# Group-norm statistics at the head of a fused attention and depthwise-convolution kernel: statistics split in two parts, more load buffers, small sums moved

## The chip, the cores and the metric

The kernel runs on one core of a Trainium2 chip. The metric is the device time in microseconds (us) of one execution, and lower is better. A profile describes one execution on the chip. Its engines are PE (TensorE, matrix products; PEld is its weight load), DVE (VectorE), ACT (ScalarE), POOL (GpSimd) and SP (SyncE, which here only starts transfers).

## What is computed

An image x of 384 channels and 192 x 192 pixels, float32, goes through two residual layers. The change lies in the first one, in the group norm and the first products behind it.

```python
# layer 0
n = groupnorm(x)                       # 32 groups of 12 channels, eps 1e-5
qkv = einsum('bchw,oc->bohw', n, w_qkv) + b_qkv      # 384 -> 1152 channels
qkv = maxpool 2x2 of qkv               # 96 x 96
qkv = depthwise 3x3 conv(qkv, w_dw) + b_dw
q, k, v = split(qkv)                   # 8 heads of 48 channels
attn = normalize(q) @ normalize(k).T * temperature   # 48 x 48 for each head
out = sum over 4 of topk_softmax(attn, kk) @ v * a
x = x + (w_proj @ upsample 2x(gelu(out)) + b_proj)
# layer 1
w_sym = mean of the four rotations of weight (7 x 7)
x = x + depthwise 7x7 conv(groupnorm(x), w_sym)
```

## The kernel before

The 384 channels are three tiles of 128 partitions (`KT`, index `kt` or `ct`). The image is cut into `NB` = 24 blocks of 8 rows (`BLK` = 1536 pixels). A group of 12 channels lies across the border between the second and the third tile, so the second tile's norm needs 8 channels of the third (`OVER`); these are loaded apart, spread over all partitions, as `xe`.

The norm is never applied to x. Its scale `rstd0` is multiplied into the rows of the weights `wq` (each row belongs to an input channel), and its mean becomes a bias: `biases` multiplies the scaled weights by `mean0` with TensorE and makes `negb` and `bdb`, which pooling borders and the depthwise taps need.

**Stage 1, statistics.** x is streamed once. For each block, `summed` (L310) runs six `bn_stats` instructions on VectorE for the first two tiles together. Blocks go from 23 down to 0. The last three (`NX`) land in `held` buffers, which are kept for stage 2; all others go through the pool `xsp` with three buffers. Then `bn_aggr` (L359) makes channel means and variances of all 24 blocks, and small matmuls against 0/1 matrices (`total`, L316) sum them over groups: first the group means (`gs_mid`, results `mids`), then moments about them (`gs`, from `ds`), from which `normed` makes `rstd0`; POOL takes the power -1/2 (L335). ScalarE scales the first two tiles of `wq` (L382). Only then the third tile's blocks are streamed in the same way, in pairs; its last block, 0, is kept apart from the aggregate of the 23 others.

**Begun products.** While the third tile's statistics run, TensorE multiplies the first two tiles of the kept blocks by the scaled weights: 24 sums of 512 pixels (`begun_qk`, L389), each two matmuls, each matmul two instructions in the trace[...]. Twenty are parked in SBUF by ScalarE (L395), the last four stay in their PSUM buffers. When the third tile's `rstd0` is there, VectorE scales the first third of its weights (L433) and ScalarE the rest (L434).

**Stage 2, q and k.** For each block, `pooled` (L553) makes the products, VectorE takes the 2 x 2 maximum into a ring of rows (L561) and runs nine taps for each tile (L601, L603), and `products` transposes and sums q by k (L621, L630). For block 0 and a part of block 1 only the third tile's product is added to the begun sums. `biases` is called after the first two tiles of block 0. POOL writes expanded 7 x 7 weights to memory meanwhile (`weights`), behind the third `rstd0`. Stage 3 makes v, the attention and the projection (L816, L903, L927), stage 4 the 7 x 7 convolution with matmuls (L1332 to L1343).

Order. A tile framework places every instruction on its engine's queue; each engine works through its queue in order. `tc.keep_in_program_order` pins matmuls to the order of the program, otherwise the planner chooses, by when it thinks that operands are there; `tc.issue_after(i)` holds an instruction behind another. The small sums over weights (`sumd` L442, `w7h` L171, `w7s` L174 and L177, `sumw` L1230) have nothing in their code that holds them back, and the planner put them among the first statistics on VectorE. SP starts the x loads, ScalarE the weight loads. A load also waits until the earlier load that used the same of eight completion semaphores has landed.

Of the kernel before, what the change touches and what calls it, by code (L numbers as in the profile page):

```python
# [13 lines left out]
P = 128  # L14
C = 384
# [63 lines left out]
def conv_preact_d2(  # L79
# [91 lines left out]
    nc.vector.tensor_tensor(w7h, w7f, w7f[:, :, ::-1], ALU.add)  # L171
    w7hv = w7h.rearrange("p t (a b) -> p t a b", b=KS)
    for i in range(KS):
        nc.vector.tensor_tensor(  # L174
            w7s[:, :, i, :], w7hv[:, :, i, :], w7hv[:, :, :, KS - 1 - i], ALU.add
        )
    nc.vector.tensor_scalar_mul(w7s, w7s, 0.25)  # L177
# [76 lines left out]

    psx = ExitStack()
# [29 lines left out]
    with tc.tile_pool(name="stp", bufs=1) as stp, tc.tile_pool(name="xsp", bufs=3) as xsp:  # L285
# [4 lines left out]
        xe = stp.tile([P, EN], F32, name="xe")  # L290
# [15 lines left out]
        nc.gpsimd.memset(whole[:, 0:OVER], 0.0)  # L306

# [4 lines left out]
        def total(name, n, terms):  # L312

            ps = ptr.tile([P, C], F32, name=name, tag="tr")
            for i, (lhs, rhs) in enumerate(terms):
                nc.tensor.matmul(ps[:, 0:n], lhs, rhs, start=(i == 0), stop=(i == len(terms) - 1))  # L316
            return ps[:, 0:n]
# [4 lines left out]
        def moments(dst, mv, mid):  # L322

            nc.vector.tensor_tensor(dst[:, 0:1], mv[:, 0:1], mid, ALU.subtract)
            nc.vector.tensor_tensor(dst[:, 1:2], dst[:, 0:1], dst[:, 0:1], ALU.mult)
            nc.vector.tensor_tensor(dst[:, 1:2], dst[:, 1:2], mv[:, 1:2], ALU.add)

        def normed(kt, ps, mid):
# [5 lines left out]
            nc.vector.scalar_tensor_tensor(rstd, g[:, 1:2], GN_EPS, rstd, ALU.add, ALU.subtract)  # L334
            last = nc.gpsimd.tensor_tensor(rstd, rstd, halfneg[:, 0:1], ALU.pow).ins  # L335
            nc.vector.tensor_tensor(mean0[:, kt : kt + 1], mid, g[:, 0:1], ALU.add)
            return last

        for b in reversed(range(NB)):
            if b < NX:  # L340
                xb = held[b][:, 0:TWO]
            else:
                xb = xsp.tile([P, TWO, BLK], F32, name=f"xs{b}", tag="xs")
# [6 lines left out]
        mv = stp.tile([P, KT, 2], F32, name="mv0")  # L350
        mve = stp.tile([P, 2], F32, name="mve")
        mids = stp.tile([P, KT + 1], F32, name="mids0")
        ds = stp.tile([P, KT, 2], F32, name="ds0")
        de = stp.tile([P, 2], F32, name="de")
        me = stp.tile([P, 1], F32, name="me")
        nc.vector.bn_aggr(mve, ste.rearrange("p n s -> p (n s)"))
        nc.vector.tensor_scalar_mul(me, mve[:, 0:1], 1.0 / EP)
        for kt in range(TWO):
            nc.vector.bn_aggr(mv[:, kt, :], st[:, kt].rearrange("p n s -> p (n s)"))  # L359
        means = [mv[:, kt, 0:1] for kt in range(TWO)]  # L360
        terms = [
            [(sel(0, 0), means[0]), (sel(1, 0), means[1])],
            [(sel(0, 1), means[0]), (sel(1, 1), means[1]), (shared[:, 0:P], me)],
            [(of, means[1]), (ones, me)],
        ]
        for k, i in ((0, 0), (1, 1), (KT, 2)):
            ps = total(f"gs_mid0_{k}", 1, terms[i])
            nc.vector.tensor_scalar_mul(mids[:, k : k + 1], ps, 1.0 / GC)
        for kt in range(TWO):
            moments(ds[:, kt], mv[:, kt], mids[:, kt : kt + 1])  # L370
        moments(de, mve, mids[:, KT : KT + 1])
        nc.vector.tensor_scalar_mul(de, de, 1.0 / EP)
        terms = [
            [(sel(0, 0), ds[:, 0]), (sel(1, 0), ds[:, 1])],
            [(sel(0, 1), ds[:, 0]), (sel(1, 1), ds[:, 1]), (shared[:, 0:P], de)],
# [3 lines left out]
        nc.vector.tensor_copy(chmean[:, 0:TWO], mv[:, 0:TWO, 0])  # L379
# [3 lines left out]
        keep = tc.keep_in_program_order  # L383
        for i, (b, ct, g) in enumerate(begun_qk):
# [14 lines left out]

        kt = TWO
        for b in [*range(NB - 2, NX, -2), NX, *reversed(range(1, NX))]:
            n = 2 if b > NX else 1
            if b < NX:
# [4 lines left out]
            nc.sync.dma_start(xb, xv[:, kt, b * BLK : (b + n) * BLK])  # L410
            summed(kt, b, n, xb)
        loaded = nc.sync.dma_start(held[0][:, kt], xv[:, kt, 0:BLK]).ins
        mvm, mvl = [stp.tile([P, 2], F32, name=f"mv0_{i}") for i in range(2)]
        dm, dl = [stp.tile([P, 2], F32, name=f"ds0_{i}") for i in range(2)]
        mid = mids[:, kt : kt + 1]
        nc.vector.bn_aggr(mvm, st[:, kt, SUB:, :].rearrange("p n s -> p (n s)"))
        ps = total(
            "gs_mid0_2", 1,
            [(sel(1, 2), means[1]), (shared[:, P:], me), (whole, mvm[:, 0:1])],
        )  # L420
        nc.vector.tensor_scalar_mul(mid, ps, 1.0 / GC)
        moments(dm, mvm, mid)
        nc.vector.tensor_scalar_mul(dm, dm, (NB - 1) / NB)
        summed(kt, 0, 1, held[0][:, kt])
        nc.vector.bn_aggr(mvl, st[:, kt, 0:SUB, :].rearrange("p n s -> p (n s)"))
        moments(dl, mvl, mid)
        nc.vector.scalar_tensor_tensor(ds[:, kt], dl, 1.0 / NB, dm, ALU.mult, ALU.add)
        ps = total(
# [995 lines left out]
```

## Time and profile before

| | us |
|---|---|
| median of 3 runs | 2841.81 |
| lowest and highest run | 2838.41, 2848.71 |
| the profiled execution | 2858.62 |
| its span, first to last instruction | 2856.9 |
| VectorE waits for wd, for w7t | 8.29, 4.48 |
| aggregates of all 24 blocks begin | 119.86 |
| first begun product on TensorE | 132.14 |
| last begun product ends | 175.34 |
| TensorE continues with the third tile | 182.45 |
| biases reach VectorE | 197.10 |
| mean granted TensorE clock | 0.983 |

Times below the span's row are counted from the start of the span, in the profiled execution. In the page, "busy" is the time in which an engine had an instruction under way; a line such as `L310 DVE` names line 310 of the kernel before and the engine. A bracket behind an instruction is the idle time before it and what ended it. In tables by stretches, each engine has its busy time and, in brackets, its instructions; the last three columns are the granted TensorE clock as a share of full speed, the busy share of the 16 DMA engines, and GB/s.

### The profile page before, as it was taken

To read this page: it belongs to the slowest core of one execution; us is meant where nothing else is said; L and a number is where in the kernel's file an instruction comes from. 1 tells how busy PE (TensorE), PEld (TensorE's weight loads), DVE (VectorE), ACT (ScalarE), POOL (GpSimd) and SP (SyncE) were. 2 spreads that over 40 slices of the span, in tenths; PEclk is the share of its full clock that TensorE was granted. 3 is DMA by queue.
4 is the path that set the end of the run, shared out by engine and by line. 5 is a ranking of instruction groups with operands and counts; after the bars stand their busy time and mean duration, and the time that the engine had idled before them with its cause. 6 is when DMAs were issued, how large, how long until landed. Compare 5 with 4: busy or idle time off the path is not lost.

```text
span 2856.9 us, 25452 instructions
## 1 busy us (share of the span) xinstructions
PE 2651.4 (93%) x8669; PEld 1585.7 (56%) x8669; DVE 2359.4 (83%) x3380; ACT 870.5 (30%) x1635; POOL 750.3 (26%) x874
## 2 busy tenths in 40 slices
PE   0299999999999999999899999999999699999997
PEld 0144444444445444444556656666666477777776
DVE  6979887887878878778688887888889679888886
ACT  0031111111111111111202232232323467777775
POOL 1024443100000000000102230010101467878785
PEclk9999999999999999999999999999999799999999
DMA  8886666301101011000335998576675899999997
GB/s 331 357 293 240 223 225 217 134 33 57 43 34 66 34 52 48 34 33 1 134 101 184 332 366 283 178 240 197 210 243 193 299 321 357 371 370 367 372 367 244
DMA packets 236401, 584.52 MB, mean 205 GB/s; under 512 B 16704, under 2 KB 168112, under 8 KB 219504
## 3 DMA queue, kind: packets, MB, share of 16 engines
q1 hardware_dynamic: 175344, 286.77, 29.2%
q0 software_dynamic: 37376, 148.85, 15.1%
q10 hardware_dynamic: 23552, 147.27, 13.7%
q8 instruction: 69, 1.13, 0.2%
q14 instruction: 60, 0.49, 0.0%
HBM read 374.47 MB, written 208.21 MB: 204 GB/s over the span
## 4 chain that ended last, share of the span: by engine, by line
PE 87%; DVE 6%; DMA 5%; POOL 1%; issue 1%; ACT 0%; SPq 0%; ACTq 0%; POOLq 0%; DVEq 0%
PE pq L553 36%; PE pv L816 19%; PE pc L1332 6%; PE pc L1343 6%; PE pc L1337 6%; PE pr L927 4%; PE po L903 3%; DMA xs<-in_x_dram 2%; PE grams L630 2%; PE tr L621 2%; DVE qk L603 2%; PE pq_begun L389 2%; DVE st L310 1%; DMA xv<-in_x_dram 1%; DVE vb L850 1%; DMA sd<-sx 1%
## 5 line engine op out<-in xcount | busy, mean ns | idle before, releaser
L553 PE MATMUL pq<-xq,wq 128*128 128x512 f32 x2268 | 990.7, 592 | 0.0
L553 PEld LDWEIGHTS pq<-xq,wq 128*128 128x128 f32 x2268 | 422.9, 190 | 492.2 <-issue 446.1
L603 DVE SCALAR_TENSOR_TENSOR qk<-ring,wd,qk 128x384 f32<-128x384 f32 x1152 | 674.0, 612 | 20.9 <-ACT ring L590 7.1
L816 PE MATMUL pv<-xv,wq 128*128 128x384 f32 x1728 | 567.0, 488 | 10.6 <-DMA xv<-in_x_dram 9.3
L816 PEld LDWEIGHTS pv<-xv,wq 128*128 128x128 f32 x1728 | 328.5, 191 | 238.2 <-DVE rows L822 8.6
L561 DVE TENSOR_REDUCE ring<-pq 128x128 f32<-128x512 f32 x428 | 293.7, 687 | 192.3 <-PE pq L553 191.7
L1356 DVE TENSOR_SCALAR apart<-pc,rb 32x576 f32<-32x576 f32 x384 | 312.2, 813 | 87.1 <-PE pc L1343 65.5
L1354 ACT ACTIVATE apart<-pc,rb 32x576 f32<-32x576 f32 x384 | 281.4, 733 | 143.0 <-PE pc L1343 138.2
L850 DVE SCALAR_TENSOR_TENSOR vb<-rows,wd,vb 128x576 f32<-128x576 f32 x384 | 313.1, 817 | 11.2
L1343 PE MATMUL pc<-aux,h 128*128 128x288 f32 x768 | 250.7, 408 | 3.5 <-POOL aux L1265 2.7
L1332 PE MATMUL pc<-main,w 128*128 128x288 f32 x768 | 251.9, 409 | 0.9 <-issue 0.3
L961 DVE TENSOR_TENSOR sx<-xr,y 128x576 f32<-128x576 f32 x192 | 217.6, 1174 | 41.0 <-ACT y L935 23.9
L1337 PE MATMUL pc<-main,w 128*128 128x288 f32 x768 | 250.7, 408 | 0.0
L612 ACT ACTIVATE junk<-qk 128x384 f32<-128x384 f32 x144 | 75.3, 523 | 540.9 <-DVE qk L603 540.9
L1302 POOL COPY res<-apart 128x1152 f32<-128x1152 f32 x96 | 224.0, 2361 | 40.9 <-ACT apart L1354 27.8
L713 POOL MEMSET lower<- 128x2304 f32 x1 | 2.0, 2018 | 871.3 <-PE grams L630 871.3
L1002 POOL DMA_DIRECT2D sd<-sx x96 | 72.3, 756 | 512.5 <-DVE sx L961 491.1
L822 DVE TENSOR_REDUCE rows<-pv 128x192 f32<-128x768 f32 x144 | 137.5, 955 | 64.6 <-PE pv L816 64.6
L1343 PEld LDWEIGHTS pc<-aux,h 128*128 128x128 f32 x768 | 145.7, 190 | 47.0 <-POOL aux L1265 3.5
L1332 PEld LDWEIGHTS pc<-main,w 128*128 128x128 f32 x768 | 145.5, 191 | 44.9 <-PE pc L1343 2.7
L1197 DVE SCALAR_TENSOR_TENSOR w<-eye,sb,w 128x512 f32<-128x512 f32 x96 | 168.8, 1797 | 1.5
L1337 PEld LDWEIGHTS pc<-main,w 128*128 128x128 f32 x768 | 146.5, 191 | 41.9
(210 smaller groups left out, 2321.0 us busy)
## 6 DMA issues: line engine op xcount, KB each, us to landing
sd<-sx POOLq DMA_DIRECT2D x96, 600.0 KB, 10.0
xv<-in_x_dram SPq DMA_DIRECT2D x144, 384.0 KB, 4.9
xr<-in_x_dram SPq DMA_DIRECT2D x48, 1152.0 KB, 14.8
out_dram<-res SPq DMA_DIRECT2D x192, 288.0 KB, 11.4
main<-sd ACTq DMA_DIRECT2D x46, 1200.0 KB, 10.0
xq<-in_x_dram SPq DMA_DIRECT2D x21, 2304.0 KB, 8.5
w<-wt ACTq DMA_DIRECT2D x46, 1024.0 KB, 7.0
xs<-in_x_dram SPq DMA_DIRECT2D x24, 1536.0 KB, 8.5
```

The costliest lines, as they stand in the source:

```text
L553: nc.tensor.matmul(ps, wq[:, kt, ct * P : (ct + 1) * P], rows[:, kt, :, g * 64 : (g + 1) * 64], start=(kt == 0), stop=(kt == KT - 1), skip ...
L561: nc.vector.tensor_reduce(t[:, r0 : r0 + PR, 1 + g * 32 : 1 + (g + 1) * 32], ps.rearrange("p (h a w b) -> p h w a b", h=PR, a=2, b=2), AX. ...
L603: nc.vector.scalar_tensor_tensor(dst, src, w, dst, ALU.mult, ALU.add)
L816: nc.tensor.matmul(ps[:, u, 0 : RB * HW], wq[:, kt, o : o + P], xb[:, kt, u, :], start=(kt == 0), stop=(kt == KT - 1),)
L850: pin(nc.vector.scalar_tensor_tensor(dst, src, w, dst, ALU.mult, ALU.add))
L961: nc.vector.tensor_tensor(bass.AP(flat.tensor, flat.offset + at(e) + a * RUN, [flat.ap[0], [JP, NT], [1, NJ], [at(f) - at(e), 2]],), xq[:, ...
L1302: keep(nc.gpsimd.tensor_copy(res[:, k], apart[:, :, k].rearrange("p e n -> p n e")))
L1332: nc.tensor.matmul(acc, w[:, i, 0:P], main[:, i, :, 0:NJ], start=True, stop=False)
L1337: nc.tensor.matmul(acc, w[:, i, P : 2 * P], main[:, i, :, 1 : 1 + NJ], start=False, stop=False,)
L1343: nc.tensor.matmul(acc, h[:, i], aux[:, i, :, 0:NJ], start=False, stop=True,)
L1354: keep(nc.scalar.mul(dst, src, scale))
L1356: keep(nc.vector.tensor_scalar_mul(dst, src, scale))
```

## The change

- The statistics of the first two tiles are aggregated in two parts: the first 21 blocks before the last three are summed, then the last three alone. The group means that moments are taken about come from the first part; both parts' moments are weighted by their share of blocks and added. The third tile does the same (21 and 3 blocks instead of 23 and 1).
- `xsp` has five buffers instead of three, and `xe` uses one of them instead of its own.
- The sums of the 7 x 7 weights move from VectorE to POOL. `sumd`, `bpm` and `sumw` are held behind the third tile's last VectorE step of the norm (`settled`).
- All small matmuls of `total` are pinned, and the last 3 of the 24 begun sums come behind the third tile's group-mean matmuls.
- All three thirds of the third tile's weights are scaled by ScalarE, in three instructions.
- The bias products are split: after a zeroing matmul, those of q and k for the first two tiles (12 of 27) run before the third tile's scale is there; the rest stays in `biases`.
- The constants `z` and `zero` become one tile in another pool.

```diff
-    nc.vector.tensor_tensor(w7h, w7f, w7f[:, :, ::-1], ALU.add)
+    nc.gpsimd.tensor_tensor(w7h, w7f, w7f[:, :, ::-1], ALU.add)
...
-        nc.vector.tensor_tensor(
+        nc.gpsimd.tensor_tensor(
             w7s[:, :, i, :], w7hv[:, :, i, :], w7hv[:, :, :, KS - 1 - i], ALU.add
         )
-    nc.vector.tensor_scalar_mul(w7s, w7s, 0.25)
+    nc.gpsimd.tensor_scalar_mul(w7s, w7s, 0.25)
...
-    with tc.tile_pool(name="stp", bufs=1) as stp, tc.tile_pool(name="xsp", bufs=3) as xsp:
+    with tc.tile_pool(name="stp", bufs=1) as stp, tc.tile_pool(name="xsp", bufs=5) as xsp:
...
-        xe = stp.tile([P, EN], F32, name="xe")
+        xe = xsp.tile([P, TWO, BLK], F32, name="xe", tag="xs")
+        xe = xe.rearrange("p k n -> p (k n)")[:, 0:EN]
...
+        def aggregate(kt, lo, hi, name):
+
+            mv = stp.tile([P, 2], F32, name=f"mv0_{kt}_{name}")
+            nc.vector.bn_aggr(mv, st[:, kt, lo * SUB : hi * SUB, :].rearrange("p n s -> p (n s)"))
+            return mv
...
+        def both(kt, most, mid):
+
+            last = moments(aggregate(kt, 0, NX, "last"), mid, f"{kt}_last")
+            nc.vector.scalar_tensor_tensor(most, last, NX / NB, most, ALU.mult, ALU.add)
+            return most
...
         for b in reversed(range(NB)):
+            if b == NX - 1:
+                most[:TWO] = [aggregate(kt, NX, NB, "most") for kt in range(TWO)]
...
+                for k, i in ((0, 0), (1, 1), (KT, 2)):
+                    ps = total(f"gs_mid0_{k}", 1, terms[i])
+                    nc.vector.tensor_scalar_mul(mids[:, k : k + 1], ps, 1.0 / GC)
+                de = moments(mve, mids[:, KT : KT + 1], "e")
+                nc.vector.tensor_scalar_mul(de, de, 1.0 / EP)
+                dm = [moments(most[kt], mids[:, kt : kt + 1], f"{kt}_most") for kt in range(TWO)]
+                for d in dm:
+                    nc.vector.tensor_scalar_mul(d, d, rest0)
...
+        ds = [both(kt, dm[kt], mids[:, kt : kt + 1]) for kt in range(TWO)]
...
+        for i in range(len(spots) + 1):
+            begin(i)
...
-        for b in [*range(NB - 2, NX, -2), NX, *reversed(range(1, NX))]:
+        for b in [*range(NB - 2, NX, -2), NX, *reversed(range(NX))]:
             n = 2 if b > NX else 1
+            if b == NX - 1:
+                most = aggregate(kt, NX, NB, "most")
+                ps = total(
+                    "gs_mid0_2", 1,
+                    [(sel(1, 2), means[1]), (shared[:, P:], me), (whole, most[:, 0:1])],
+                )
+                nc.vector.tensor_scalar_mul(mid, ps, 1.0 / GC)
+                dm = moments(most, mid, "2_most")
+                nc.vector.tensor_scalar_mul(dm, dm, rest0)
+                for i in range(len(spots) + 1, len(begun_qk)):
+                    begin(i)
...
+        d = both(kt, dm, mid)
+        ps = total("gs0_2", 2, [(sel(1, 2), ds[1]), (shared[:, P:], de), (whole, d)])
+        stats0, settled = normed(kt, ps, mid)
...
+        bias_ps = ptr.tile([P, C], F32, name="bias_ps", tag="tr")
...
+        for ct in range(2 * KT):
+            for kt in range(TWO):
+                leave(ct, kt)
-    nc.vector.tensor_scalar_mul(wq[:, kt, 0:C], wq[:, kt, 0:C], rstd0[:, kt : kt + 1])
-    nc.scalar.mul(wq[:, kt, C:], wq[:, kt, C:], rstd0[:, kt : kt + 1])
+    for i in range(3):
+        w = wq[:, TWO, i * C : (i + 1) * C]
+        nc.scalar.mul(w, w, rstd0[:, TWO : TWO + 1])
...
-    nc.vector.tensor_reduce(sumd, wd, AX.X, ALU.add)
+    with tc.issue_after(settled):
+        nc.vector.tensor_reduce(sumd, wd, AX.X, ALU.add)
...
             for ct in range(CT):
-                for kt in range(KT):
...
+                for kt in range(TWO if ct < 2 * KT else 0, KT):
+                    leave(ct, kt)
```

`begin(i)` holds the body of the old loop over `begun_qk` (two matmuls, and the copy to SBUF for the first 20); `leave(ct, kt)` is one pinned bias matmul into `bias_ps`, accumulating. On VectorE the order after the change has no statistics between the first part's aggregates and its scaled moments, and the sums `sumd`, `bpm` and `sumw` stand just ahead of the first pooling; SP's order is the same.

## The prediction

> **What bounds the kernel now.** I read the page first, for the share of each engine and the 40 slices.
>
> ```profile
> span 2856.9 us, 25452 instructions
> ...
> PE 2651.4 (93%) x8669; PEld 1585.7 (56%) x8669; DVE 2359.4 (83%) x3380; ACT 870.5 (30%) x1635; POOL 750.3 (26%) x874
> ...
> PE   0299999999999999999899999999999699999997
> ```
>
> TensorE is busy in every slice but the first two and a few joints. A change that removes no matmul of weight can only move the moment from which TensorE runs without a pause. So the question is the first 200 us, and there the views by engine count. VectorE's timeline, which shows start, busy time, instruction and the idle time before it:
>
> ```profile
> 7.41 2.86 DVE L349 BATCH_NORM_STATS2 ste<-xe 128x6 f32<-128x384 f32 x6 [5.14 <-DMA xe<-in_x_dram]
> 18.57 0.24 DVE L442 TENSOR_REDUCE sumd<-wd 128x9 f32<-128x81 f32 x1 [8.29 <-DMA wd<-in_wdw_dram]
> ...
> 26.07 0.31 DVE L171 TENSOR_TENSOR w7h<-w7t 128x147 f32<-128x147 f32 x1 [4.48 <-DMA w7t<-in_w_dram]
> ...
> 104.99 14.95 DVE L310 BATCH_NORM_STATS2 st<-xs 128x6 f32<-128x512 f32 x24 [0.41 <-DMA xs<-in_x_dram]
> 119.86 4.05 DVE L359 BATCH_NORM_AGGREGATE mv<-st 128x2 f32<-128x432 f32 x2
> ```
>
> Two small sums over weights stand in VectorE's order ahead of the statistics of x, and it stood still 8.29 and 4.48 us for their transfers. No x buffer came free meanwhile. The table by stretches (the last two columns are the share of the 16 DMA engines and GB/s) shows what that cost:
>
> ```profile
> 18.50:28.70 10.20, 0.00 (x0) 0.00 (x0) 5.59 (x19) 1.28 (x1) 0.00 (x0) 1.00 0.49 162
> ...
> 40.00:50.00 10.00, 0.00 (x0) 0.00 (x0) 8.74 (x15) 0.00 (x0) 0.00 (x0) 1.00 1.00 393
> ...
> 100.00:110.00 10.00, 0.00 (x0) 0.00 (x0) 9.07 (x16) 0.00 (x0) 0.00 (x0) 1.00 1.01 420
> 110.00:120.00 10.00, 0.00 (x0) 0.00 (x0) 9.79 (x18) 0.00 (x0) 0.00 (x0) 1.00 1.02 425
> ```
>
> The loads stood half idle at 18.5 to 28.7; with three buffers they then ran at 378 to 405 GB/s, and at 420 to 425 only at the end, where three loads into the kept blocks need no buffer. The chain of waits (start, length) tells what follows:
>
> ```profile
> 98.17 18.09 DMA xs<-in_x_dram
> ...
> 119.94 3.98 DVE mv L359 x2
> ...
> 132.14 43.20 PE pq_begun L389 x96
> ...
> 182.45 5.88 PE pq_begun L553 x8
> ...
> 190.05 7.02 PE bias_ps L573 x50
> ```
>
> From the last load to the first product 15.9 us pass (116.26 to 132.14). The begun products end at 175.34, then TensorE waits for the third tile's statistics to 182.45, and the biases stand on it until 197.06. At 197.10 VectorE has the biases and starts its backlog of pooling and taps; TensorE has no gap beyond 0.94 us after that. So the mark that I compare is "biases on VectorE": 197.10 us. What it gains, the end gains.
>
> **The change part by part.**
>
> *Weight sums moved.* The sumd, w7h/w7s and sumw work leaves the head of VectorE's order. The w7 part goes to POOL, which is idle from 8.3 to 130.5 us and next does the power of the first rstd; nine small operations there after w7t lands (26 us) are 90 us early. sumd and sumw (0.24 and 0.30 us) come after the third rstd, where VectorE waits over 2 us for TensorE; at worst they reach 0.5 us into that wait. So VectorE stops only for x.
>
> *Five buffers.* They change nothing before 18.5 us: in both orders SP's second x load waits for xe to land and its third for a small bias load (11.1 us in the table of SP's waits), since both reuse a completion semaphore. xe now takes one of the five. Two x blocks have landed by 18.5 us (moved: 8 us at 284 and 10.5 us at 369 GB/s, 6.1 MB, the sum of xe, wq and two blocks). Block three, issued at 18.5, lands at about 24.5 (6 us for a single load, like xe's 6.6). From there I need the pace of an x block of 1.573 MB. Bounds: 4.02 us (the 20 blocks whose statistics end between 39.5 and 119.94 us) if buffers do not matter, 3.73 us (14.95/4, VectorE's own pace, met at 420 to 425 GB/s) if they do. I take 3.8, near the row with as many loads in flight.
>
> [...]
>
> *First statistics in two parts.* Of 24 blocks 21 are aggregated before the last three. Statistics of block 21 end at 24.5 + 3.7 + 18 x 3.8 = 96.6. Then VectorE works on the first part: two aggregates of 21/24 x 1.99 us (3.5), a wait for 12 TensorE instructions at 0.23 us (2.8; the 10 in this chain took 2.28), means, squares and scaling (1.3): 7.6 us with no statistics beside it. That is new on VectorE, and what queues behind it are the three last blocks; their loads go into kept buffers and are not delayed. 18 statistics of 0.61 us follow: 115.2. From there: two short aggregates (0.7; the 128x18 one took 0.23 and the 128x414 one 2.02), moments and weighting 0.75, 10 TensorE instructions 2.3, norm and rstd 0.6, POOL's power 0.6, ScalarE's scaling 0.95: begun products start at 121.2, against 132.14. That is 10.9 us, nearly all from the loads; the split itself cuts the tail from 12.2 to 6.0 us behind the last statistics and gives that back in the 7.6 us.
>
> *Third tile.* VectorE returns to statistics at 115.2 + 4.6 = 119.8; five blocks wait in the buffers by 123, so it is not held by loads. 63 + 1 statistics (39.0), an aggregate of 378 elements (1.85): its first part is ready at A = 160.7. TensorE has 21 of the 24 begun sums done at 121.2 + 38.0 = 159.2 and waits 1.5 us for A: a new stall, as the last three sums now stand behind this matmul. They take 5.2 us and end at A + 5.5; VectorE's remaining 8 statistics, aggregate and moments end at A + 6.4. Then gs (0.4), norm (0.55), power (0.6 with its wait), and ScalarE's first third (about 0.5; 0.93 for 768 columns): A + 8.6. The old step was VectorE's L433, 2.30 us, so moving it saves 1.8. In that gap TensorE now does 13 of the bias products, 26 instructions at 0.095 us (21 in 2 us at full clock, next fence): until A + 9.3. They fill the wait and overrun by 0.7.
>
> The clock, from the stretches again (column before DMA share):
>
> ```profile
> 180.00:182.00 2.00, 0.00 (x0) 0.00 (x0) 1.91 (x1) 0.93 (x1) 2.00 (x2) 0.51 0.00 0
> ...
> 190.00:192.00 2.00, 2.00 (x21) 2.00 (x19) 0.69 (x1) 1.13 (x2) 0.00 (x0) 1.00 0.98 293
> ...
> 194.00:196.00 2.00, 2.00 (x11) 2.00 (x10) 0.00 (x0) 0.00 (x0) 0.00 (x0) 0.50 1.00 285
> ```
>
> It fell 4.7 us after the last wide matmul (175.3) and again some 4 us into the bias products (189.9): small products do not hold it. My new gap without wide matmuls is 3.8 us (A + 5.5 to A + 9.3). [...] If it falls, 3.4 to 6.8 us at half speed cost 1.7 to 3.4 us. I charge nothing and keep 3.4 for the range.
>
> *Restart to biases.* Before 14.65 us (182.45 to 197.10): 12 matmuls, partly at half clock (5.88 + 1.72), and 50 bias instructions in 7.02. After: 12 x 0.43 = 5.2, then 30 instructions at 0.095 = 2.9: A + 17.4 = 178.1. TensorE's half clock until 200 us goes too, but VectorE bounds there: 0, at most 1.6.
>
> Costed at nothing: z and zero merged and moved (memsets before any data), the extra zeroing matmul (counted in the 26), chmean and bpm moved (VectorE waits there), SP's order (unchanged), POOL's first weight pieces (they start with the third rstd and shift along).
>
> **Sum.** First products 10.9 earlier; begun sums to restart 48.8 instead of 50.3 (1.5); restart to biases 8.1 instead of 14.65 (6.5): 19 us. The profiled execution took 2858.62 us (span 2856.9 and 1.7 around it), 16.8 over the median of 2841.81. The chain shows why: one x load of 26.69 us at 1692.89 made a round of the loop 63.9 us instead of 50.35. That is 13.5 us which the median need not hold; none of it is in the first 200 us. Rounding the gain to 18.5, the profiled one would give 2840 and the median 2823.
>
> **The rivals.**
> *Loads no faster (11%).* At 4.02 us a block, block 21 ends at 100.6: 4 us lost; with a clock drop at the restart, 3.4 more. Gain 11.6: 2830, within 0.5%. For it: the DMA share reads 1.00 already at 393 GB/s. Against: 425 with more in flight.
> *The head start is given back (4%).* TensorE reaches later blocks earlier, and if their xq loads or the backlog of VectorE held it, the gain would shrink to the bias part, 6.5 us: 2835. Against: the backlog's work is unchanged and starts when the biases do, and xq loads land in 8.5 us against a block of 51.
> *Slower (3%).* More loads in flight could disturb each other. All 34 blocks' worth after the second must land; with pace p the last does at 20.5 + 34p and the biases follow 13.9 us later, so the change loses from p = 4.8 us (328 GB/s), and loses 14 us at 5.2 (302 GB/s): 2856. No stretch between 40 and 120 us is under 378.
>
> **Numbers.** The likeliest case has 82%: 2823, own range 2817 to 2828 (pace 3.73 to 3.95, clock kept). About 0.5%, 14.2 us, is what a measurement of this kernel can tell from no change; the runs spread over 10 us. The border is 2827.6: of the likeliest case 4 of the 82 lie inside it, and so do the first two rivals: faster 0.78, same 0.19, slower 0.03. With the runs' spread, the range is 2813 to 2833.
>
> **What would show it.** Right: no VectorE wait on wd or w7t; DMA share at 1.0 from 20 us; first begun product near 121; a wait of 1 to 2 us before gs_mid's last product at 160; restart near 170 with the clock at 1.00; biases near 178; the same 51 us per block after. Wrong: block statistics still 4 us apart, begun products after 125, a clock of 0.5 at the restart, or a new TensorE gap between 180 and 260.

## The result and the profile after

The changed kernel takes 2823.41 us (median of 4 runs, 2822.68 to 2826.64) against 2842.36 us (median of 4, 2838.41 to 2848.71). The ratio is 0.9933, with a 95% interval of 0.9913 to 0.9953. The profiled execution has a span of 2822.3 us at a mean granted clock of 0.986.

First the page of the changed kernel: span, busy time of the engines, and TensorE's 40 slices.

```profile
span 2822.3 us, 25466 instructions
...
PE 2640.1 (94%) x8671; PEld 1581.2 (56%) x8671; DVE 2331.7 (83%) x3382; ACT 871.1 (31%) x1637; POOL 752.8 (27%) x884
...
PE   0399999999999999999899999999998699999997
```

TensorE is busy for nearly as long as before, 2640 us against 2651; what shrank is the time before it runs without a pause. VectorE's timeline of the changed kernel (start, busy time, instruction, idle time before it and what ended that):

```profile
26.08 3.66 DVE L318 BATCH_NORM_STATS2 st<-xs 128x6 f32<-128x512 f32 x6 [3.97 <-DMA xs<-in_x_dram]
30.00 14.95 DVE L318 BATCH_NORM_STATS2 st<-xs 128x6 f32<-128x512 f32 x24 [0.26 <-DMA xs<-in_x_dram]
46.02 52.58 DVE L318 BATCH_NORM_STATS2 st<-xs 128x6 f32<-128x512 f32 x84 [1.06 <-DMA xs<-in_x_dram]
98.51 3.56 DVE L337 BATCH_NORM_AGGREGATE mv_most<-st 128x2 f32<-128x378 f32 x2
...
105.85 10.77 DVE L318 BATCH_NORM_STATS2 st<-xs 128x6 f32<-128x512 f32 x18
116.54 0.64 DVE L337 BATCH_NORM_AGGREGATE mv_last<-st 128x2 f32<-128x54 f32 x2
...
120.71 37.47 DVE L318 BATCH_NORM_STATS2 st<-xt 128x6 f32<-128x512 f32 x63
...
158.69 1.84 DVE L337 BATCH_NORM_AGGREGATE mv_most<-st 128x2 f32<-128x378 f32 x1
...
180.45 0.17 DVE L624 TENSOR_TENSOR negb<-bias_ps,bq 128x9 f32<-128x9 f32 x1 [2.55 <-PE bias_ps L470]
```

No wait on wd or w7t is left. From 46.02 us on, 14 blocks pass in one piece at 3.76 us each, where before there was a wait of 0.3 to 1.1 us in every few blocks. The pause for the first part is 7.3 us (98.51 to 105.85). The third tile's 63 statistics run without a wait. The biases reach VectorE at 180.45 us instead of 197.10.

The loads behind it, in the table by stretches of the changed kernel:

```profile
18.50:28.70 10.20, 0.00 (x0) 0.00 (x0) 6.23 (x11) 1.28 (x1) 0.00 (x0) 1.00 0.84 304
...
40.00:50.00 10.00, 0.00 (x0) 0.00 (x0) 8.73 (x16) 0.00 (x0) 0.00 (x0) 1.00 1.02 416
100.00:110.00 10.00, 3.25 (x14) 3.13 (x14) 7.44 (x24) 0.00 (x0) 0.00 (x0) 1.00 1.02 426
```

304 GB/s stand where 162 were, and 416 where 393 were. TensorE's timeline of the changed kernel around the joint:

```profile
122.34 38.06 PE L423 MATMUL pq_begun<-xs,wq 128*128 128x512 f32 x84 [2.16 <-ACT wq L415]
...
160.90 5.40 PE L423 MATMUL pq_begun<-xs,wq 128*128 128x512 f32 x12
...
167.40 2.82 PE L470 MATMUL bias_ps<-mean,wq 128*128 128x1 f32 x24
170.08 5.38 PE L604 MATMUL pq_begun<-xs,wq 128*128 128x512 f32 x8
175.29 1.88 PE L604 MATMUL pq<-xs,wq 128*128 128x512 f32 x4
177.01 3.40 PE L470 MATMUL bias_ps<-mean,wq 128*128 128x1 f32 x30
180.28 8.81 PE L604 MATMUL pq<-xs,wq 128*128 128x512 f32 x16
```

Begun products start 9.8 us earlier and the third tile's product (the restart) 12.4 us earlier. But the eight instructions at 170.08 take 5.38 us, 0.67 each, where the 12 at the end of the begun sums took 0.45 each. The table by stretches of the changed kernel says why (third column from the right: granted clock):

```profile
168.00:170.00 2.00, 2.00 (x20) 2.00 (x20) 0.33 (x3) 1.44 (x3) 2.00 (x2) 1.00 0.00 0
170.00:172.00 2.00, 2.00 (x5) 0.96 (x6) 0.00 (x0) 0.19 (x1) 1.94 (x8) 0.57 0.00 0
172.00:174.00 2.00, 2.00 (x3) 0.72 (x3) 0.98 (x2) 0.59 (x1) 1.99 (x3) 0.58 0.32 94
...
180.00:182.00 2.00, 2.00 (x7) 0.97 (x7) 0.51 (x3) 1.35 (x6) 0.00 (x0) 0.63 0.99 299
182.00:184.00 2.00, 2.00 (x4) 0.91 (x3) 0.83 (x2) 2.00 (x8) 0.00 (x0) 0.52 1.00 285
```

The clock falls to half at the restart, for some 3.4 us, and again at 180.5. The prediction had charged nothing for that. In steps of 0.25 us the two falls stand at 170.27 and 180.5:

```profile
170.00:170.25 0.25, 0.25 (x3) 0.25 (x4) 0.00 (x0) 0.19 (x1) 0.25 (x1) 1.00 0.00 0
170.25:170.50 0.25, 0.25 (x1) 0.14 (x1) 0.00 (x0) 0.00 (x0) 0.25 (x1) 0.54 0.00 0
...
180.25:180.50 0.25, 0.25 (x3) 0.25 (x3) 0.05 (x1) 0.00 (x0) 0.00 (x0) 1.00 1.00 311
180.50:180.75 0.25, 0.25 (x1) 0.05 (x1) 0.22 (x2) 0.10 (x1) 0.00 (x0) 0.52 0.97 295
```

Behind the biases the gain stays: the first product of v (stage 3) starts at 1378.49 us instead of 1395.42, so 16.9 us earlier. The two spans differ by 34.6 us. The lead of one execution over the other is 17.4 us through the first third of stage 3, jumps to 30.9 us at the slow x load of 26.69 us that the prediction set aside, and grows by another 4 us in stage 4, which was not traced.

### The profile page after: what moved, and what is told of

Its sections match the earlier page's. It is cut to its first block, busy times and chain, and to the rows that moved or that the text cites. A ratio compares the mean times of both kernels' runs of the same rounds, so it can differ in the third digit from the quotient of the medians.

```text
span 2822.3 us, 25466 instructions
## 1 busy us (share of the span) xinstructions
PE 2640.1 (94%) x8671; PEld 1581.2 (56%) x8671; DVE 2331.7 (83%) x3382; ACT 871.1 (31%) x1637; POOL 752.8 (27%) x884
## 3 DMA queue, kind: packets, MB, share of 16 engines
q10 hardware_dynamic: 23552, 147.27, 13.9%
## 4 chain that ended last, share of the span: by engine, by line
PE 88%; DVE 6%; DMA 4%; POOL 1%; ACT 1%; issue 0%; ACTq 0%; POOLq 0%; SPq 0%; DVEq 0%
PE pq L604 38%; PE pv L858 20%; PE pc L1387 6%; PE pc L1376 6%; PE pc L1381 6%; PE pr L970 4%; PE po L946 3%; DVE st L318 2%; DMA xs<-in_x_dram 2%; PE grams L674 2%; PE tr L665 2%; DVE sx L1004 1%; DVE vb L892 1%; DVE qk L647 1%; DMA bp<-in_bproj_dram 1%
## 5 line engine op out<-in xcount | busy, mean ns | idle before, releaser
L892 DVE SCALAR_TENSOR_TENSOR vb<-rows,wd,vb 128x576 f32<-128x576 f32 x384 | 313.1, 817 | 11.2
L1024 ACT ACTIVATE wq<-sx,negmid 128x1152 f32<-128x1152 f32 x96 | 120.6, 1257 | 96.9 <-DVE sx L1004 92.8
```

What stands on the lines that cost most here:

```text
L892: pin(nc.vector.scalar_tensor_tensor(dst, src, w, dst, ALU.mult, ALU.add))
```

## The experiments

Three marks are compared in every kernel: the start of the begun products, the biases on VectorE, and the first product of v. They are read from one execution of each kernel. They are steadier than the total: the changed kernel was run again beside the last experiments and repeated its marks within 1 us, while its ratio came out as 0.9947 instead of 0.9933. The profiles show where the total's spread comes from. From the first product of v to the last one 764 us pass in eight of the fourteen profiled executions and 768 to 777 in the other six, and stage 4 takes 589 to 599 us; neither goes with a part of the change. Ratios are to the kernel before on the same chip, which had a median of 2852.96 us beside "three buffers" to "biases together", 2841.24 beside the single additions, "half the biases forward" and "small loads moved", and 2840.80 beside the other four. "Third part ready" is the end of the aggregate of the third tile's first part; where before and its kin have another cut (23 blocks), it is the end of that one. In the last two rows "biases" are those of q and k alone; those of v follow some 10 us later.

| kernel | begun products | third part ready | restart | biases | first v | us | ratio (95%) |
|---|---|---|---|---|---|---|---|
| before | 132.14 | 173.94 | 182.45 | 197.10 | 1395.42 | 2842.36 | 1 |
| before + five buffers | 125.23 | 165.13 | 176.28 | 190.89 | 1389.84 | 2835.34 | 0.9980 (0.9974–0.9987) |
| before + sums moved | 123.32 | 167.00 | 174.74 | 189.41 | 1387.82 | 2831.26 | 0.9968 (0.9955–0.9981) |
| before + both | 121.59 | 161.48 | 172.94 | 187.57 | 1384.89 | 2829.79 | 0.9966 (0.9958–0.9975) |
| changed | 122.34 | 160.53 | 170.08 | 180.45 | 1378.49 | 2823.41 | 0.9933 (0.9913–0.9953) |
| changed, again | 121.42 | 159.60 | 169.63 | 180.00 | 1377.81 | 2825.49 | 0.9947 (0.9928–0.9966) |
| three buffers | 125.14 | 165.62 | 176.40 | 186.77 | 1384.63 | 2840.97 | 0.9959 (0.9936–0.9981) |
| sums back | 126.56 | 164.77 | 174.61 | 184.98 | 1386.56 | 2838.88 | 0.9955 (0.9931–0.9979) |
| no first split | 120.83 | 157.91 | 169.04 | 179.41 | 1377.19 | 2832.58 | 0.9926 (0.9898–0.9955) |
| biases together | 121.58 | 159.77 | 169.44 | 182.85 | 1381.95 | 2833.52 | 0.9940 (0.9916–0.9964) |
| half the biases forward | 121.50 | 159.69 | 170.55 | 180.94 | 1378.39 | 2822.58 | 0.9938 (0.9923–0.9953) |
| small loads moved | 120.80 | 158.99 | 169.56 | 179.93 | 1376.49 | 2822.88 | 0.9938 (0.9924–0.9953) |
| biases mixed in | 121.41 | 159.60 | 169.00 | 178.09 | 1374.06 | 2822.14 | 0.9936 (0.9912–0.9959) |
| mixed, no split, loads moved | 119.84 | 156.92 | 167.72 | 176.81 | 1373.28 | 2819.32 | 0.9926 (0.9909–0.9942) |

**Three buffers.** The changed kernel with the old pool:

```diff
-    with tc.tile_pool(name="stp", bufs=1) as stp, tc.tile_pool(name="xsp", bufs=5) as xsp:
+    with tc.tile_pool(name="stp", bufs=1) as stp, tc.tile_pool(name="xsp", bufs=3) as xsp:
...
-        xe = xsp.tile([P, TWO, BLK], F32, name="xe", tag="xs")
-        xe = xe.rearrange("p k n -> p (k n)")[:, 0:EN]
+        xe = stp.tile([P, EN], F32, name="xe")
```

> The changed kernel with three x buffers in place of five, the short-tile block xe in a tile of its own as before. Theory (the buffers carry the faster pace of the loads): an x block takes about 4.0 us again instead of 3.76, so block 21's statistics end near 102 us instead of 98.59, begun products start near 126, the third tile's statistics are held by loads too; biases on VectorE near 187 us instead of 180.45, time about 6 us above the changed kernel's 2823. Rival (the pace comes from VectorE no longer stopping for weights, buffers are worthless): biases within 1 us of 180.45 and the same time.

VectorE's timeline of this kernel:

```profile
49.58 11.17 DVE L317 BATCH_NORM_STATS2 st<-xs 128x6 f32<-128x512 f32 x18 [0.66 <-DMA xs<-in_x_dram]
...
77.70 14.92 DVE L317 BATCH_NORM_STATS2 st<-xs 128x6 f32<-128x512 f32 x24 [1.28 <-DMA xs<-in_x_dram]
93.97 7.42 DVE L317 BATCH_NORM_STATS2 st<-xs 128x6 f32<-128x512 f32 x12 [1.34 <-DMA xs<-in_x_dram]
```

The waits on x are back. Block 21 ends at 101.4 us, begun products start some 3 us later, and the third tile's statistics wait for loads too: its first part is ready 5 to 6 us later. Biases come at 186.77: the theory's 187. The rival, that buffers are worthless, falls.

**Sums back.** The changed kernel with the small sums at VectorE's head again:

```diff
-    nc.gpsimd.tensor_tensor(w7h, w7f, w7f[:, :, ::-1], ALU.add)
+    nc.vector.tensor_tensor(w7h, w7f, w7f[:, :, ::-1], ALU.add)
...
-    with tc.issue_after(settled):
-        nc.vector.tensor_reduce(sumd, wd, AX.X, ALU.add)
+    nc.vector.tensor_reduce(sumd, wd, AX.X, ALU.add)
```

(w7s likewise, and bpm and sumw without their holds.)

> The changed kernel with the small weight sums (sumd, w7h, w7s, sumw) back at their old place in VectorE's order, and bpm unheld. Theory: VectorE stops again for wd and w7t, some 8 us and 4 us; five buffers fill meanwhile, but VectorE needs 3.66 us for a block and loads 3.76, so it can make up little of the lost time; block 21 ends near 104, biases near 186.5, time +6 us over the changed kernel. Rival (five buffers absorb the stops, because loads set the pace): biases 180.5 to 181.5, time +0 to +1.

VectorE's timeline of this kernel:

```profile
18.46 0.24 DVE L495 TENSOR_REDUCE sumd<-wd 128x9 f32<-128x81 f32 x1 [8.30 <-DMA wd<-in_wdw_dram]
...
28.89 0.31 DVE L171 TENSOR_TENSOR w7h<-w7t 128x147 f32<-128x147 f32 x1 [7.40 <-DMA w7t<-in_w_dram]
...
31.53 71.29 DVE L318 BATCH_NORM_STATS2 st<-xs 128x6 f32<-128x512 f32 x120
```

VectorE stops as before, but then 20 blocks run at 3.56 us each, its own pace, without a single wait: the buffers had filled. Ahead of that it stood still for 8.3 us (wd) and 7.4 us (w7t, 21.49 to 28.89), the changed kernel for 7.9 us in all, waiting for x (3.42, 0.54 and 3.97). Of these 8 us more, 4 to 5 remain at the begun products and at the biases (184.98). The theory's 186.5 was 1.5 us too high, the rival's 181 too low: five buffers hide a part, not all. Behind the biases this kernel lost about 3.5 us more up to v; some 1.6 us of that fall together with a further half-clock stretch at 195.7 to 199.1 (41 products took 19.54 us where the changed kernel's pace would give 17.9). The rest was not traced.

**Each alone, and both.** The kernel before with five buffers; with the sums moved; with both. The edits are the same lines in the other direction.

> The kernel before with five x buffers (xe in the pool) and nothing else. Theory (a buffer free during VectorE's stops lets the loads run on, and VectorE then works the backlog off at its own pace): VectorE still stops for wd and w7t until about 31 us, then 23 blocks' statistics follow at 3.6 us each without a wait; the 24th block ends near 113.5 instead of 119.94, biases near 189.5 instead of 197.10, time -7 us. Rival (buffers are worth something only when VectorE no longer stops): 24th block near 119, time 0 to -1 us.

> The kernel before with the small weight sums moved as in the change (w7h and w7s on GpSimd, sumd, bpm and sumw held until the third rstd), three x buffers, nothing else. Theory (VectorE without stops keeps the loads going from the start, at 4.0 us a block at worst): the 24th block ends near 112.5 instead of 119.94, biases near 189.5, time -7 us. So each of the two parts alone would bring more than half of what both bring. Rival (the stops are only what the pace of the loads at 4.0 us leaves idle): 24th block at 118 to 120, time 0 to -1 us.

> The kernel before with five x buffers and the small weight sums moved, and nothing else of the change: no split, third tile and biases as before. Theory (these two parts are the 11 us at the first products, and each alone already brought 6.2 and 7.7 us at the biases, so they overlap by some 3): 24th block's statistics end near 109.5, begun products at 121, biases at 186 instead of 197.10, time -10 to -11 us; what is left to the changed kernel's 180.45, some 5.5 us, is the third tile's scaling on ScalarE and the bias products ahead of the restart. Rival (they add up or more: 14 us): biases at 183, time -14 us.

Alone they bring 6.2 and 7.7 us at the biases, together 9.5, not 13.9. Both work on the same loss, the loads that stood still while VectorE did: at 18.5 to 28.7 us the kernel before moved 162 GB/s, with the buffers alone 324 and with the sums alone 319. The 24th block's statistics end at 112.9 us with the buffers and 111.0 with the sums (113.5 and 112.5 were expected), and at 109.3 with both. The rivals, that either is worth nothing alone or that they add up, fall. In the time: 0.9980 and 0.9968 alone, 0.9966 together; that both beat the moved sums alone is seen in the marks only.

The last run also shows what the rest of the change is for. With both, the third part is ready 12.5 us earlier than before, but the restart comes only 9.5 us earlier. TensorE's timeline of the kernel before with both:

```profile
121.59 43.40 PE L392 MATMUL pq_begun<-xs,wq 128*128 128x512 f32 x96 [1.10 <-ACT wq L385]
164.83 0.50 PE L577 MATMUL bias_ps<-mean,wq 128*128 128x1 f32 x4
165.19 0.36 PE L317 MATMUL gs_mid<-mv,whole 128*128 128x1 f32 x2
...
172.94 5.56 PE L557 MATMUL pq_begun<-xs,wq 128*128 128x512 f32 x8 [3.61 <-DVE wq L436]
```

The third part was ready at 161.48; the group-mean product that waits for it started at 165.19, behind all 24 begun sums. In the changed kernel that product stands ahead of the last three sums, and starts 0.15 us after the part is ready. From the restart to the biases this kernel needs 14.63 us, as before (14.65). So in this order of adding parts the loads (buffers and sums) give 9.5 of the 16.65 us at the biases, and all the rest together 7.1: both splits of the statistics, the order on TensorE, ScalarE's scaling and the split biases. Of these only the first split and the biases are taken out alone below; the order, the scaling and the third tile's cut were not run alone. The remainder differs from the 5.5 expected because the biases came at 187.57, not 186.

The shares depend on each other. On top of the moved sums, five buffers make the third part ready 5.5 us earlier in the old order, but bring only 1.8 us at the biases (189.41 to 187.57), since the group-mean product stands behind the begun sums. In the changed order they bring 6.3 to 6.8 us (186.77 against 180.45 and 180.00). So the order is what lets the faster loads through.

**No first split.** The first two tiles' 24 blocks are aggregated once, behind the last statistics; the third tile keeps its two parts.

```diff
         for b in reversed(range(NB)):
-            if b == NX - 1:
-                most[:TWO] = [aggregate(kt, NX, NB, "most") for kt in range(TWO)]
...
-        ds = [both(kt, dm[kt], mids[:, kt : kt + 1]) for kt in range(TWO)]
+        most[:TWO] = [aggregate(kt, 0, NB, "most") for kt in range(TWO)]
...
+        ds = dm
```

> The changed kernel without the split of the statistics of the first two tiles: all 24 blocks are aggregated once, behind the last statistics; the third tile keeps its split. Theory (the split gives back ahead of the last three blocks what it saves behind them): no pause of VectorE at 98.5, last statistics end near 110 instead of 116.6, then a tail of 12 us: begun products at 122 (within 1 us), first part of the third tile ready at 159.3, biases 179.3 to 180.5, time -1 to 0 us. Rival (the split is what starts the products earlier): begun products at 128, biases and time +6 us.

VectorE's and TensorE's timelines of this kernel:

```profile
108.97 4.05 DVE L337 BATCH_NORM_AGGREGATE mv_most<-st 128x2 f32<-128x432 f32 x2
...
120.83 38.60 PE L420 MATMUL pq_begun<-xs,wq 128*128 128x512 f32 x84 [1.95 <-ACT wq L412]
```

Begun products at 120.83, biases at 179.41: 0.6 to 1.5 us earlier than with the split. The split saves 6 us behind the last statistics (11.9 from here, 5.8 with it) and pays 7.3 us in the middle of VectorE's work. So splitting the first two tiles' statistics is worth nothing here, or slightly less than nothing; the rival falls.

**Biases together.** All 27 bias products behind the restart.

```diff
-        for ct in range(2 * KT):
-            for kt in range(TWO):
-                leave(ct, kt)
...
-                for kt in range(TWO if ct < 2 * KT else 0, KT):
+                for kt in range(KT):
```

> The changed kernel with all 27 bias products behind the restart, as before, none ahead of it; only the zeroing product stays ahead. Theory: the third tile's matmul restarts about 1 us sooner (169.2 instead of 170.2), the gap without wide matmuls is near 3 us so that the granted clock may hold through the restart, but 24 more bias instructions (2.7 us) follow it: biases near 182.3, time +1.9 us. Rival (those products cost nothing where they are, and the clock's fall at the restart is what costs): clock 1.0 at the restart, biases within 0.5 us of 180.45, time +0.

TensorE's timeline and the table by stretches of this kernel:

```profile
169.44 3.70 PE L601 MATMUL pq_begun<-xs,wq 128*128 128x512 f32 x8 [1.69 <-ACT wq L484]
...
174.70 8.12 PE L470 MATMUL bias_ps<-mean,wq 128*128 128x1 f32 x54
```

```profile
170.00:172.00 2.00, 2.00 (x6) 0.93 (x5) 1.23 (x2) 0.99 (x2) 1.94 (x8) 1.00 0.00 0
...
178.00:180.00 2.00, 2.00 (x13) 2.00 (x13) 0.00 (x0) 0.00 (x0) 0.00 (x0) 0.61 1.00 295
180.00:182.00 2.00, 2.00 (x11) 2.00 (x11) 0.00 (x0) 0.00 (x0) 0.00 (x0) 0.50 1.01 307
```

The clock held at the restart, where the eight products took 3.70 us instead of 5.38, and fell at 178.43, 3.7 us into the long train of bias products. Restart 169.44, biases 182.85: 2.4 to 2.9 us later than the changed kernel, as the theory said (182.3). So the products ahead of the restart pay, although the fall comes with them.

**Half the biases forward.** The zeroing and six products go ahead of the last three begun sums, to shorten the gap without wide products.

```diff
+                for ct in range(KT):
+                    for kk in range(TWO):
+                        leave(ct, kk)
                 for i in range(len(spots) + 1, len(begun_qk)):
                     begin(i)
...
-        for ct in range(2 * KT):
+        for ct in range(KT, 2 * KT):
```

> The changed kernel with the bias products ahead of the restart spread out: the zeroing product and six of the twelve go before the last three begun sums (while TensorE waits for the third tile's first part anyway), six stay in the gap. Theory (the clock falls at the restart because the gap without wide products is 3.8 us, while 2.9 us in the run with all of them behind the restart kept it at 1.0): gap near 2.9 us, clock 1.0 at the restart, restart at about 169.4 to 170, its first four products 3.4 to 3.7 us instead of 5.4, biases near 178, time -2.5 us. Rival (the fall comes from something else than the length of the gap): clock 0.5 to 0.6 after the restart again, biases at 180 to 181, time 0.

The table by stretches of this kernel:

```profile
170.00:172.00 2.00, 1.45 (x3) 0.68 (x4) 0.29 (x1) 1.51 (x3) 1.97 (x1) 0.92 0.00 0
172.00:174.00 2.00, 2.00 (x4) 0.77 (x3) 1.10 (x2) 0.59 (x1) 1.96 (x7) 0.50 0.00 0
```

The expectation failed. The gap was 2.5 us, shorter than the 2.9 that had held, and the clock fell all the same, at 171.7, when wide products had run again for 1.1 us. And the seven products put ahead of the last three sums delayed these by 1.6 us, and with them the group sums behind them, ScalarE's scaling (169.88 instead of 168.56) and the restart, which came 0.5 to 0.9 us later. The length of the gap alone is not what decides. The first fall of each kernel, read from tables in steps of 0.25 us:

| kernel | gap without wide products | its length | clock falls at | behind the gap's end | half clock lasts |
|---|---|---|---|---|---|
| changed | 166.30–170.08 | 3.78 | 170.27 | 0.19 | 3.4 |
| no first split | 165.25–169.04 | 3.79 | 169.83 | 0.79 | 3.4 |
| changed, again | 165.84–169.63 | 3.79 | 170.43 | 0.80 | 3.4 |
| three buffers | 163.55–165.98 | 2.43 | 166.94 | 0.96 | 3.4 |
| sums back | 170.82–174.61 | 3.79 | 175.23 | 0.62 | 3.4 |
| half forward | 168.07–170.55 | 2.48 | 171.67 | 1.12 | 3.4 |
| small loads moved | 165.77–169.56 | 3.79 | 170.90 | 1.34 | 3.4 |
| biases together | 166.51–169.44 | 2.93 | not behind this gap | – | – |

(With three buffers the gap and the fall lie ahead of the last three begun sums, which took 7.09 us instead of 5.40.) All five gaps of 3.8 us had a fall behind them, and so had two of 2.4 and 2.5 us, while the one of 2.9 us had none. What else decides these tables do not show. So the run with the biases mixed in, below, does not shorten the gap but puts wide products into it.

**Small loads moved.** The ten small loads leave ScalarE's queue for GpSimd's, so that SP's third x load does not wait 11.2 us for bp's semaphore.

```diff
-    nc.scalar.dma_start(bp, bproj)
+    nc.gpsimd.dma_start(bp, bproj)
...
```

(The other nine likewise.)

> The changed kernel with the ten small loads (bq, wd, bd, bp, temp, the scalars, w7t) issued by GpSimd's queue instead of ScalarE's. Theory (SP's third x load is held 11.2 us by the landing of bp, because both reuse a completion semaphore): SP issues its first x loads at once, the third x block lands near 22 instead of 26.08, VectorE's idle time before block three goes from 4 us to under 1, everything behind comes 3 to 4 us earlier: biases near 177, time -3.5 us. Rival (the loads already fill the memory port until 18.5 us, at 284 to 370 GB/s): block three at 25 to 26, time 0 to -0.5 us.

The table by stretches of this kernel, for the two stretches that were 370 and 304 GB/s in the changed kernel:

```profile
8.00:18.50 10.50, 0.00 (x0) 0.00 (x0) 6.09 (x13) 1.28 (x1) 6.24 (x17) 1.00 0.85 329
18.50:28.70 10.20, 0.00 (x0) 0.00 (x0) 7.46 (x13) 0.00 (x0) 2.50 (x9) 1.00 1.01 410
```

The hole behind 18.5 us closed (410), but the loads before it fell to 329, with 70 to 176 GB/s from 15.0 to 16.8 us. From 8 to 28.7 us 7.64 MB moved (10.5 us at 329 and 10.2 us at 410 GB/s) instead of 6.99, which is worth 1.6 us. Block two came 2.1 us later, block three's statistics began at 24.78 instead of 26.08, biases at 179.93. Neither expectation: the theory's 3.5 us is out, a gain of 0.6 to 1.5 us at the begun products was there, and nearly all of it ended behind TensorE's begun sums, which were done 1 us after the third part was ready. Why the loads sagged there stays open.

**Biases mixed in.** Three zero products of 384 columns and two bias products stand in the gap; sixteen bias products of q and k stand two or three behind each wide product of the restart, the nine of v one behind each later one.

```diff
+        for i in range(3):
+            wide(i == 0)
+            if i < 2:
+                leave(*first[i])
+        spread = first[2:] + [(ct, TWO) for ct in range(2 * KT)]
...
+                    if b == 0 and ct < 5:
+                        keep(mm)
+                        beside(ct)
```

> The changed kernel with the bias products mixed among wide ones. The gap before the restart holds three zero products of 384 columns and two bias products; the other sixteen bias products of q and k go two or three behind each of the six wide products of the restart; the nine of v go one behind each later wide product, with their own small sums on VectorE. [...]

The table by stretches of this kernel:

```profile
170.00:172.00 2.00, 2.00 (x16) 1.52 (x14) 1.10 (x2) 0.59 (x1) 1.94 (x8) 1.00 0.00 0
172.00:174.00 2.00, 2.00 (x11) 1.30 (x11) 0.98 (x2) 0.69 (x2) 1.99 (x4) 1.00 0.63 184
...
180.00:182.00 2.00, 2.00 (x8) 1.04 (x7) 2.00 (x4) 2.00 (x9) 0.00 (x0) 1.00 0.98 285
182.00:184.00 2.00, 1.89 (x7) 1.08 (x8) 2.00 (x5) 1.72 (x4) 0.00 (x0) 1.00 1.01 287
```

The clock stayed at 1.00 from 160 to 192 us, the first kernel in which it did. The forecast had been a clock of 1.00 from 162 to 190 us, the restart at about 169.7, the biases of q and k at 178 to 178.5 and 2 to 3 us less than the changed kernel. Restart 169.00, biases 178.09, and at the first v product the gain has grown to 3.8 us against the changed kernel run beside it. VectorE shows where the rest came from: it is busy for all of 180 to 186 us, where in the changed kernel it waited for products at half clock (0.51 and 0.83 us busy in the two stretches of 2 us above). So the forecast of the marks holds. The medians differ by 3.4 us, but the ratios' intervals overlap. Since v's bias products moved away from the joint as well, the clock's own share of the 3.8 us is not separated.

**Changed once more, and all together.**

> The changed kernel once more, unedited, beside the others on this chip. Every theory: -18 to -20 us against the kernel before; clock at the restart low for 3.4 us as in its first profile if the gap of 3.8 us alone decides.

> The changed kernel without the split of the first two tiles' statistics, with the small loads on GpSimd's queue, and with the mixed bias products of the run before: every piece that was even or better. Theory: split 1.0 us, small loads 0.5 to 1.5 us, clock 2 to 2.5 us, which partly hide behind each other: biases at 176.5 to 177.5, time -3 to -4 us against the changed kernel, near 2820. Rival (TensorE's 21 begun sums end after the third tile's first part is ready, so that what the loads gain waits there): biases at 178, time -2 us.

The changed kernel's clock fell again at 170.43. Its ratio of 0.9947 means some 15 us, a little under the expectation. The combination has the biases at 176.81 and the first v at 1373.28, 4.5 us ahead of the changed kernel beside it, with the clock at 1.00 from 160 to 192 us; its median of 2819.32 is the lowest of all. Beside the changed kernel's interval its own (0.9909 to 0.9942) still overlaps, so the 4.5 us are shown by the marks, and the 6.2 us between the medians are only suggested.

## Why the prediction was right, point by point

The path was right: TensorE runs earlier because VectorE and the loads no longer stop, and what is gained at the biases is kept to stage 3. The time came out as predicted, 2823.41 for 2823.0, but that closeness is luck. At the biases the gain is 16.65 us, not 19, and 16.9 at the first v product. The further 2 us between the medians (18.95) come behind it, where stages 3 and 4 vary by more than that from one profiled execution to the next; when the changed kernel ran again, the medians were 15.3 us apart.

- *The sum's first term* (begun products 10.9 us earlier): 9.8 in the first profile, 10.7 in the second. The pace of an x block was sized rightly, 3.76 for 3.8; the run with three buffers shows that this pace needs the five. But 3.73 us is not VectorE's own pace, as the prediction had it: with the sums back it works a block in 3.56, so in the changed kernel the loads still set the pace (416 GB/s is 3.78 us a block). The third block landed at 26.06, not 24.5: it was issued at 18.98, and a single load took 7.1 us and not 6. The same load had taken 7.0 us in the kernel before.
- *The split gives back what it saves*: 7.3 us for the predicted 7.6 in the middle, 5.8 us (116.54 to 122.34) for 6.0 behind. Removing it made the marks about 1 us earlier.
- *The second term* (begun products to restart, 48.8 us): 47.7. The predicted stall of 1.5 us at the third part did not come. TensorE was done with the 21 sums at 160.4 since it began 1.1 us late, and the part was ready at 160.53. ScalarE's three thirds took 1.63 us from 168.56 on, so the first was there near 169.1, as predicted, and the bias products overran it by 1 us, for 0.7.
- *The third term* (restart to biases, 8.1 us): 10.4. This is the step that failed. Twelve wide instructions took 6.9 us (170.08 to 177.01) instead of 5.2, since the clock was at half for 3.4 us, and the second train of 30 took 3.4 instead of 2.9. The prediction charged nothing for its gap of 3.8 us. The rows of the kernel before held a sign against that: between those of 190 and 194 us that it showed stands `192.00:194.00 2.00, 2.00 (x19) 2.00 (x18) 0.00 (x0) 0.00 (x0) 0.00 (x0) 0.92 1.02 295`, with a clock of 0.92, so the second fall came near 193.7, 3.8 us after wide products had ended at 189.9, which is just as long as the new gap. All five runs with a gap of 3.8 us fell. The 3.4 us that the range keeps for a fall would be the cost of 6.8 us at half clock, which is how long both periods of the kernel before lasted (180.04 to 186.87 and 193.69 to 200.52). No run shows a loss of 3.4 us at the restart: in the changed kernel the clock was at half for 3.4 us, and the twelve instructions took 1.7 us more.
- *The rivals.* "Loads no faster" is the run with three buffers: it costs 6.3 to 6.8 us at the biases, and did not happen. The head start was not given back: 16.65 us at 180 us and 16.9 at 1378. Nothing slowed the loads in the rows shown (304, 416 and 426 GB/s against 162, 393 and 420).
- *Its own signs.* Begun products near 121, the restart near 170 and no wait on wd or w7t came. The DMA share at 18.5 to 28.7 us was 0.84, not 1.0, and a clock of 0.5 at the restart, which stood among the signs of being wrong, came.

Where the errors met: the third term took 2.3 us, the late third block 1.1, and the missing stall gave 1.1 back. That leaves 2.3 us less gain at the biases than predicted; that the medians hide this is chance.

## What to carry to other kernels

Buffers and the removal of a consumer's stops repaired the same loss here; either alone was worth more than half of both, so price the second by what the first leaves, and look whether the next engine's order lets the gain through. A mark that every engine passes (here: biases on VectorE) tells 1 us where the total tells 5. When small products fill a gap on TensorE, read the granted clock behind it in steps of 0.25 us: mixing small ones among wide ones, with three wide zero products in the gap, kept the clock at 1.00 here, and gave 2 us at the joint and 3.8 us in all at the first v product.

## What was not expected of the hardware

- A clock that falls when wide products run again: in the seven kernels of the table it fell 0.2 to 1.3 us after they had begun. So the fall is easily put down to the products that are running; the eight of the restart ran without one in the kernel with biases together, in 3.70 us.
- Gaps of 2.4 and 2.5 us with a fall behind them, where one of 2.9 us had none. That small products (128 x 1, 0.11 us each) do not keep the clock up was expected, and seen: in the kernel with biases together, 54 instructions of them began at 174.70 us, and the clock fell at 178.43. In both kernels with three zero products of 384 columns in the gap it stayed at 1.00 to 192 us.
- Moving ten small loads to another queue raised the bytes of 8 to 28.7 us by only 9%: a hole of 304 GB/s at 18.5 to 28.7 us closed, and one of 329 opened in front of it.
